# Experts sorted pair by pair, and a build-time scheduler with measured durations

## The chip, the cores and the metric

The kernel runs on one core of one Trainium2 chip, in float32 throughout. A core has TensorE (PE in the profile: matmuls and transposes, results in eight PSUM banks), VectorE (DVE), ScalarE (ACT), GpSimd (POOL) and SyncE (SP, which here only issues DMAs). The engines run their own instruction lists in order and meet at semaphores. The metric is the device time of one execution in microseconds (us), the median of several runs.

## The reference, cut to what matters

A tensor x of 16 sequences, 256 tokens each, 128 features, goes through four layers. Each layer normalises x, adds an attention, normalises again and adds a feed-forward part:

```
x = L0_attn_x                                    # (16, 256, 128)
x = x + L0_attn(ln(x)); x = x + L0_ffn(ln(x))    # 16 heads of 64, causal with distance bias, 2 null keys; gelu 128-512-128
x = x + L1_attn(ln(x)); x = x + L1_ffn(ln(x))    # 16 heads of 8, causal; gated 128-512, two 512-512 gelu layers, 512-128
x = x + L2_attn(ln(x)); x = x + L2_ffn(ln(x))    # 16 heads of 64, no mask; 8 experts
x = x + L3_attn(ln(x)); x = x + L3_ffn(ln(x))    # 16 heads of 8, causal, window 128; token shift and gates
```

The part that the change touches most is the third feed-forward layer, in which each token goes to the one expert with the highest gate value:

```
logits = xf @ gate_w.T + gate_b
top1 = argmax(logits, axis=-1)
for e in range(8):
    h = relu(xf @ w1[e].T + b1[e])
    y = h @ w2[e].T + b2[e]
    out = out + where((top1 == e)[:, None], y, 0)
```

## The kernel before

**A planner writes the order.** The source does not issue instructions as it goes along. It hands *steps* to a planner (class Plan, lines 66 to 219). A step has an engine, a rank p (a small number means wanted early), an assumed duration in ns, a function that emits its instructions, and the values that it reads (r), writes (w) or changes (m). run (line 129) then simulates the engines at build time and takes one step after the other; the order in which it takes them is the order in each engine's instruction list. Nothing is reordered on the chip. If a duration is assumed wrongly, the list is still correct, only the engine then waits.

What run looks at:

- A step can be taken when its inputs are there in the plan's time, and when its homes have a free place. A home is a set of buffers: "t" is the eight PSUM banks, "probs" six softmax tiles, "r" eight 128x512 tiles, "w" and "xs" three expert weight and row buffers, and so on. SEEN and TAIL add the delay between engines.
- Steps of a rank more than WINDOW = 12 beyond the *front* are held back. The front is the lowest rank of a PE step not yet taken (by_rank, line 132, and front, line 163).
- Among the steps that an engine could start within 40 ns of its earliest, it takes the lowest rank (line 190).
- PE steps have a mode: "T" is a plain full-array matmul or transpose, "S" and "O" use half-height or half-width tiles of the array, "S4" and "O4" quarter tiles. A step in another mode than the last counts SWITCH = 130 ns more (line 187).
- A copy out of a PSUM bank (evac, line 386; engine "AD") may run on ACT or on DVE. copies (line 377) gives the two assumed durations; whichever engine gets to it first in the plan takes it. Its rank is that of its matmul less 8.

**The layers.** Layer 0 has ranks from A0 = 0, 16 per sequence; layer 1 from A1, 12 per sequence; layer 2 from A2, 16 per sequence; layer 3 from A3, 12 per sequence. Layers overlap where ranks and data allow. In the layers with heads of 64 a sequence has four units (wide_unit, line 445) of four heads: scores (S), softmax on DVE and ACT, the division by the sum on POOL, transposes (T), products (O). In those with heads of 8 a sequence has three units (narrow_unit, line 532): scores (S4), first on DVE (line 553: adds the mask, takes the maximum, in one instruction per head and 128 queries), second on ACT (line 559: the exponential), transposes (T), products (O4). After each second sequence the feed-forward step of that pair follows; mix (line 1297) is that of layer 3.

**The experts.** Tokens are in two parts of eight sequences (four pairs) each; a part has its own sorted array of rows in DRAM. gate (line 1074) runs for each pair after its attention: it normalises into a tile of home "r", computes logits, a one-hot choice (oh), the count of earlier tokens with the same choice (ct), and on POOL a running total over the 128-token tiles (sofar). When all four pairs of a part are through, route (line 1121) runs once for the part: blocks_of works out how many blocks of 128 rows each expert needs and where they begin, places the row of each token (idx), owners the expert of each block (owni). Then 16 scatters (line 1157) on POOL, one per 128 tokens, write the normalised rows to their places in ex_rows by an indirect DMA. Then 23 blocks (line 1165): SP fetches the block's expert weights (line 1173) and rows (line 1174), PE transposes the rows (line 1178), two matmul steps with a relu between, and SP writes the result. Then 16 gathers on POOL (back, line 1205; indirect DMA at line 1210, addition at line 1215) bring the results back to x.

Their ranks, in experts (line 1234): part 0 route A2 + 153, scatters from A2 + 156, blocks from A2 + 178 every 2, gathers from A2 + 230; part 1 route A3 + 22, scatters from A3 + 23, blocks from A3 + 40 every 1.5, gathers from A3 + 70. The second part thus runs among the attention of layer 3, which begins at A3 with the first eight sequences; sequences 8 to 15 need the second part's gathers.

Of the kernel before, what the change touches and what calls it, by code (L numbers as in the profile page):

```python
# [15 lines left out]
P = 128  # L16
# [23 lines left out]
EX_PARTS = ((0, 4), (4, 8))  # L40
EX_BLOCKS = [4 * (z - a) + 7 for a, z in EX_PARTS]
# [25 lines left out]
class Plan:  # L67
# [5 lines left out]

    SEEN = {"PE": 80, "ACT": 60, "DVE": 60, "POOL": 110, "SP": 100}
# [54 lines left out]
    def run(self):  # L129
        free = dict.fromkeys(self.SEEN, 0.0)  # L130
        ready = {e: [] for e in free}
        by_rank = sorted((s for s in self.steps if s.eng[0] == "PE"), key=lambda s: (s.p, s.no))
# [27 lines left out]
        while left:  # L160
# [11 lines left out]
            for e, steps in ready.items():  # L172
                could = []
                for t, s in steps:
                    if s.p > front + window:
                        continue
                    k = places(s)
                    if k is None:
                        continue
                    t = max(t, k + self.SEEN[e] if k else 0.0, free[e])  # L180
                    could.append((t, s.p, s.no, s))
# [3 lines left out]
                if e == "PE":  # L185
                    low = min(c[1] for c in could if c[0] <= soon + 40)
                    could = [(t + (self.SWITCH if s.mode != mode else 0), p, n, s) for t, p, n, s in could
# [41 lines left out]
def preln_d4_kernel(ctx: ExitStack, tc: tile.TileContext, x_in, vecs, rows, bv2, nullk, nullv,  # L229
# [147 lines left out]
    def copies(n):  # L377
        return (0.83 * n + 42, 1.04 * n + 66)
# [11 lines left out]
    def layernorm(b, p, xn, at, times=1, behind=()):  # L390
# [22 lines left out]
        step("DVE", p, 560, stats, r=[X[b]], w=[ln])  # L413
        step("POOL", p, 980, scale, m=[ln])
# [119 lines left out]
    def narrow_unit(q, b, u, st, mask, mkey):  # L534
# [12 lines left out]
        for g in range(4):  # L547
# [14 lines left out]
            step("DVE", q + 1 + 0.7 * g, nh * (1.22 * w + 125), first, r=[s[g], mkey], w=[nm, pr, k])  # L562
# [81 lines left out]
    A0, A1, A2, A3 = 0, 4 * 4 * B, 4 * 4 * B + 4 * 3 * B, 4 * 8 * B + 4 * 3 * B  # L644
# [37 lines left out]
    step("DVE", -15, 800, null1, w=["nss"])  # L682
# [90 lines left out]
    def first0(p, u, k, bank, pr, j, nm):  # L773
# [5 lines left out]
        step("DVE", p, 730, f, r=[bank, f"bias{u}"], w=[pr, nm])  # L779
# [139 lines left out]
    def feed1(g):  # L919
        lo = A1 + 12 * (2 * g + 1) + 8 + 16  # L920
# [7 lines left out]
        for c in range(4):  # L928
# [14 lines left out]
            step("DVE", p - 8, 1270, gated, r=[pa, pb, "s1"], m=[th], w=[h[c]])  # L943
# [48 lines left out]
    def to_experts(e):  # L992
# [5 lines left out]
        for part in range(2):  # L998
            n = EX_BLOCKS[part]
            nt = n - 7  # L1000
            for name, shape, dt in (("oh", [nt, 8], F32), ("ct", [2, nt, 8], F32), ("sofar", [nt + 1, 8], F32),
                                    ("big", [n * 8], F32), ("nb", [3, 8], F32), ("pos", [nt], F32), ("idx", [nt], I32),
                                    ("own", [n], F32), ("owni", [n], I32)):
                late[name, part] = xq.tile([P] + shape, dt, tag=f"{name}{part}", name=f"{name}{part}x")
            nc.gpsimd.memset(late["sofar", part][:, 0, :], 0.0)

    step("SP", A1 + 70, 1000, to_w2, m=["wA"], w=["w2"], tail=15000)
    step("SP", A2 + 30, 1000, to_experts, m=["w1"], w=["late"], tail=4000)
# [5 lines left out]
    def prep2(b):  # L1014
        st = {}
        lo, hi = A2 + 16 * (b - 1), A2 + 16 * b - 2
# [45 lines left out]
    class Experts:  # L1062
# [12 lines left out]
        def gate(self, g, lo):  # L1075
# [24 lines left out]
            step("DVE", lo + 5, 1150, chosen, r=[ps, "late"], m=[lg], w=[oh, self.key("oh")])  # L1100
# [20 lines left out]
        def route(self, lo):  # L1121
            nt, nblk = self.nt, self.nblk

            def blocks_of(e):

                big, nb = self.tile("big"), self.tile("nb")
                c = big[:, 0:8 * nt].rearrange("p (e k) -> p e k", e=8)
                nc.vector.tensor_tensor(c, self.tile("sofar")[:, nt, :].unsqueeze(2).broadcast_to([P, 8, nt]),
                                        iota128[:, 0:nt].unsqueeze(1).broadcast_to([P, 8, nt]), ALU.is_gt)
                nc.vector.tensor_reduce(nb[:, 0, :], c, AX.X, ALU.add)  # L1130
                c = big[:, 0:64].rearrange("p (e k) -> p e k", e=8)
                nc.vector.tensor_tensor(c, before8, nb[:, 0, :].unsqueeze(1).broadcast_to([P, 8, 8]), ALU.mult)
                nc.vector.tensor_reduce(nb[:, 1, :], c, AX.X, ALU.add)
                nc.vector.tensor_tensor(nb[:, 2, :], nb[:, 0, :], nb[:, 1, :], ALU.add)
                nc.vector.tensor_scalar(nb[:, 1:3, :], nb[:, 1:3, :], float(P), None, ALU.mult)

            def places(e):
                cum = self.tile("ct")[:, 0, :, :]
                nc.vector.tensor_tensor(cum, cum, self.tile("sofar")[:, 0:nt, :], ALU.add)
                nc.vector.tensor_tensor(cum, cum, self.tile("nb")[:, 1, :].unsqueeze(1).broadcast_to([P, nt, 8]), ALU.add)  # L1140
                nc.vector.tensor_tensor(cum, cum, self.tile("oh"), ALU.mult)
                nc.vector.tensor_reduce(self.tile("pos"), cum, AX.X, ALU.add)
                nc.vector.tensor_copy(self.tile("idx"), self.tile("pos"))

            def owners(e):

                c = self.tile("big")[:, 0:8 * nblk].rearrange("p (j e) -> p j e", e=8)
                own = self.tile("own")
                nc.vector.tensor_tensor(c, iota128[:, 0:nblk].unsqueeze(2).broadcast_to([P, nblk, 8]),
                                        self.tile("nb")[:, 2, :].unsqueeze(1).broadcast_to([P, nblk, 8]), ALU.is_ge)  # L1150
                nc.vector.tensor_reduce(own, c, AX.X, ALU.add)
                nc.vector.tensor_scalar(own, own, 7.0, None, ALU.min)
                nc.vector.tensor_copy(self.tile("owni"), own)
# [287 lines left out]
```

## Time and profile before

| what | value |
|---|---|
| median of 3 runs | 2312.21 us (2311.94 to 2312.24) |
| the profiled execution's own time | 2310.75 us |
| its span, first to last instruction | 2309.1 us |
| PE busy | 2221.0 us, 96% |
| DVE busy | 1687.8 us, 73% |
| ACT busy | 1636.5 us, 71% |
| POOL busy | 1055.2 us, 46% |
| mean granted TensorE clock | 0.993 |

Busy time counts an engine as busy while an instruction of it is in flight. For PE that is not the same as working at its peak, since matmuls are pipelined and the ends are modelled. The stretches in which the layers mostly run are: layer 0 up to about 660 us, layer 1 to about 1190, layer 2 to about 1860 (experts of part 0 from 1607 to 1876), layer 3 to the end (experts of part 1 from 1937 to 2115).

### The profile page before, as it was taken

How to read it: one execution, taken by the hardware profiler on the slowest of the kernel's cores; microseconds unless marked ns; L12 is line 12 of the kernel's file. 1: busy time of each engine (PE TensorE's matmuls, PEld its weight loads, DVE VectorE, ACT ScalarE, POOL GpSimd, SP SyncE). 2: the span in 40 equal slices, each digit the busy share in tenths (PEclk: the TensorE clock that was granted, in tenths of full speed). 3: DMA queues.
4: the chain of work that ended last, by engine and by line, in shares of the span. 5: the costliest groups of instructions: out<-in, count | busy, mean ns of one | idle time of the engine just before them, and what ended most of it. 6: DMA issues, size and time to landing. Idle time of an engine off the chain costs nothing.

```text
span 2309.1 us, 50061 instructions
## 1 busy us (share of the span) xinstructions
PE 2221.0 (96%) x17039; PEld 1567.9 (68%) x17039; DVE 1687.8 (73%) x6308; ACT 1636.5 (71%) x4624; POOL 1055.2 (46%) x1985
## 2 busy tenths in 40 slices
PE   6999999999999999999999999999999999798996
PEld 3677666766776566565666677777788877586664
DVE  6898888888879665566655466767666679578996
ACT  5887877887879766677665565666665668567885
POOL 6887787877851111111112334445633483316321
PEclk9999999999999999999999999999999999899998
DMA  5000000000020000000000000000133100461000
GB/s 166 2 1 1 1 2 1 1 2 1 1 88 2 1 1 1 1 1 1 1 1 1 1 1 1 1 1 14 41 107 110 47 14 10 129 177 28 6 11 10
DMA packets 40895, 57.29 MB, mean 25 GB/s; under 512 B 4272, under 2 KB 31168, under 8 KB 40640
## 3 DMA queue, kind: packets, MB, share of 16 engines
q1 hardware_dynamic: 37840, 49.06, 7.0%
q0 software_dynamic: 2048, 4.20, 0.6%
q8 instruction: 136, 2.23, 0.4%
q10 hardware_dynamic: 752, 0.83, 0.1%
q14 instruction: 119, 0.97, 0.1%
HBM read 43.85 MB, written 10.22 MB: 23 GB/s over the span
## 4 chain that ended last, share of the span: by engine, by line
PE 75%; DVE 11%; POOL 8%; ACT 2%; issue 2%; DMA 1%; SPq 0%; POOLq 0%; DVEq 0%; ACTq 0%
PE t4x L366 8%; PE t2x L366 8%; PE t1x L366 8%; PE t0x L366 7%; PE t3x L366 7%; PE t5x L366 7%; PE t7x L366 7%; PE t6x L366 7%; PE t1x L484 1%; PE t5x L484 1%; PE t0x L484 1%; DVE probs4x L553 1%; PE t4x L484 1%; PE t2x L484 1%; PE t7x L484 1%
## 5 line engine op out<-in xcount | busy, mean ns | idle before, releaser
L441 POOL TENSOR_TENSOR x<-x,row_sb 128x256 f32<-128x256 f32 x48 | 35.1, 731 | 25.7 <-DVE xn2x L410 9.7
L473 POOL TENSOR_SCALAR probs2x<-probs2x,sums6x 128x256 f32<-128x256 f32 (+2 forms) x44 | 19.5, 459 | 47.8 <-DVE sums6x L468 25.3
L403 POOL TENSOR_SCALAR ln_rs2x<-ln_mv2x 128x2 f32<-128x2 f32 x22 | 4.6, 207 | 79.2 <-DVE ln_mv2x L399 78.5
L975 POOL TENSOR_TENSOR x<-x,sq1x 128x512 f32<-128x512 f32 x4 | 5.1, 1274 | 77.7 <-DVE sq1x L973 77.7
L370 POOL TENSOR_TENSOR ss2x<-ss2x,mhalf 128x16 f32<-128x16 f32 x11 | 33.1, 3010 | 15.5 <-DVE ss2x L728 12.0
L370 POOL TENSOR_TENSOR ss0x<-ss0x,mhalf 128x16 f32<-128x16 f32 x11 | 32.7, 2975 | 13.2 <-DVE ss0x L728 12.9
L403 POOL TENSOR_SCALAR ln_rs0x<-ln_mv0x 128x2 f32<-128x2 f32 x22 | 4.5, 207 | 74.7 <-DVE ln_mv0x L399 73.8
L473 POOL TENSOR_SCALAR probs0x<-probs0x,sums6x 128x256 f32<-128x256 f32 (+2 forms) x44 | 19.5, 457 | 36.6 <-DVE sums6x L468 36.4
L473 POOL TENSOR_SCALAR probs4x<-probs4x,sums6x 128x256 f32<-128x256 f32 (+2 forms) x40 | 17.6, 457 | 40.4 <-DVE sums6x L468 34.5
L473 POOL TENSOR_SCALAR probs4x<-probs4x,sums4x 128x256 f32<-128x256 f32 (+2 forms) x44 | 20.8, 487 | 32.2 <-DVE sums4x L468 19.5
L403 POOL TENSOR_SCALAR ln_rs4x<-ln_mv4x 128x2 f32<-128x2 f32 x23 | 4.7, 206 | 66.0 <-DVE ln_mv4x L399 65.0
L370 POOL TENSOR_TENSOR ss1x<-ss1x,mhalf 128x16 f32<-128x16 f32 x11 | 33.7, 3068 | 1.6 <-DVE ss1x L728 1.6
L370 POOL TENSOR_TENSOR ss4x<-ss4x,mhalf 128x16 f32<-128x16 f32 x10 | 29.8, 2980 | 10.1 <-DVE ss4x L728 8.2
L370 POOL TENSOR_TENSOR ss3x<-ss3x,mhalf 128x16 f32<-128x16 f32 x11 | 33.3, 3027 | 0.0
L403 POOL TENSOR_SCALAR ln_rs3x<-ln_mv3x 128x2 f32<-128x2 f32 x22 | 4.5, 206 | 62.0 <-DVE ln_mv3x L399 60.9
L473 POOL TENSOR_SCALAR probs4x<-probs4x,sums2x 128x256 f32<-128x256 f32 (+2 forms) x44 | 21.0, 492 | 25.6 <-DVE sums2x L468 20.4
L370 POOL TENSOR_TENSOR ss5x<-ss5x,mhalf 128x16 f32<-128x16 f32 x10 | 30.0, 2998 | 0.0
L975 POOL TENSOR_TENSOR x<-x,sq0x 128x512 f32<-128x512 f32 x4 | 5.1, 1279 | 54.4 <-DVE sq0x L973 54.4
L403 POOL TENSOR_SCALAR ln_rs1x<-ln_mv1x 128x2 f32<-128x2 f32 x23 | 4.7, 206 | 54.1 <-DVE ln_mv1x L399 53.0
L473 POOL TENSOR_SCALAR probs2x<-probs2x,sums2x 128x256 f32<-128x256 f32 (+2 forms) x44 | 20.8, 487 | 18.1 <-DVE sums2x L468 12.4
L473 POOL TENSOR_SCALAR probs0x<-probs0x,sums4x 128x256 f32<-128x256 f32 (+2 forms) x44 | 21.4, 500 | 15.5 <-DVE sums4x L468 15.5
L473 POOL TENSOR_SCALAR probs2x<-probs2x,sums4x 128x256 f32<-128x256 f32 (+2 forms) x40 | 19.5, 503 | 19.5 <-DVE sums4x L468 19.5
(4353 smaller groups left out, 10327.2 us busy)
## 6 DMA issues: line engine op xcount, KB each, us to landing
w0x<-in_wex_dram SPq DMA_DIRECT2D x16, 578.0 KB, 3.9
w1x<-in_wex_dram SPq DMA_DIRECT2D x15, 578.0 KB, 3.9
w2x<-in_wex_dram SPq DMA_DIRECT2D x15, 578.0 KB, 4.0
w_wA<-in_wa_dram SPq DMA_DIRECT2D x8, 512.0 KB, 6.9
ex_rows<-zero SPq DMA_DIRECT2D x2, 1472.0 KB, 10.3
x<-in_x_dram SPq DMA_DIRECT2D x8, 256.0 KB, 6.5
w_wB<-in_wb_dram SPq DMA_DIRECT2D x4, 512.0 KB, 7.5
ex_y<-bT1x SPq DMA_DIRECT2D x19, 64.0 KB, 3.4
```

Source lines behind the costliest of these rows:

```text
L366: nc.tensor.matmul(o, lhsT, rhs, start=start, stop=stop, **kw)
L370: nc.gpsimd.tensor_tensor(t, t, mhalf[:t.shape[0]].broadcast_to([t.shape[0], n]), ALU.pow)
L403: nc.gpsimd.tensor_scalar(ln.t[2], ln.t[1][:, :, 1], LN_EPS, 1.0, ALU.add, ALU.mult)
L441: step("POOL", p, 670, lambda e: nc.gpsimd.tensor_tensor(x_of(b), x_of(b), row_over(name, 2), ALU.add), m=[X[b]])
L473: nc.gpsimd.tensor_scalar(pr.t[:, j, a:z], pr.t[:, j, a:z], sums.t[:, i:i + 1], 1.0, ALU.mult, ALU.mult)
L484: nc.tensor.transpose(t.t[:, i * P:(i + 1) * P], probs[k // 2].t[:, k % 2, a:a + P], ident)
L553: nc.vector.tensor_tensor_reduce(pr.t[:, g % 2, c], s[g].t[:, c], m, -1.0, 3.0e38, ALU.add, ALU.min, nm.t[:, j:j + 1])
L975: step("POOL", lo + 30, 1300, lambda e: nc.gpsimd.tensor_tensor(x, x, ys.t.rearrange("p (c d) -> p c d", d=D), ALU.add), r=[ys, "w1"], m=xx)
```

## The change

Three things are done at once.

**The scheduler.** Steps of mode "T" no longer count for the front: it is the lowest rank of an S, O, S4 or O4 step not yet taken. A PE step of another mode is taken to start at the later of its own readiness and the engine's free time plus 130 ns; before, the 130 ns were added to its readiness. A copy that may run on either engine has its rank raised by SHY = 8 where DVE chooses (not where ACT does). Assumed durations change: copies, layer-norm statistics 560 to 788 ns, its scale 980 to 1070, first of the narrow units per instruction from 1.22 w + 125 to 1.04 w + 78 (for w = 256: 437 to 344; for w = 128: 281 to 211), first of layer 0 730 to 557, gated 1270 to 1380, the mix's difference 1300 to 1000, and one of 800 to 780.

**The sort.** route is replaced by place, which runs for each pair right behind its gate. State is kept between pairs in nb (9 rows of 8 numbers in place of 3) and own: blocks that each expert has so far, the end of all blocks so far, the block that each expert has open. A pair's tokens first fill the open block of their expert and go on in new blocks at the end. The number of blocks (23 a part) stays. A pair's four scatters follow its place at once.

**Ranks.** With first[l, b] the first rank of sequence b in layer l (the same numbers as before: A2 + 16 b, A3 + 12 b): place at first[2, b] + 29 and + 30, scatters at first[2, b] + 30, where b is the pair's second sequence. Blocks of part 0 from A2 + 157 (178 before) every 2, its gathers all at A2 + 207 (230 to 245 before). Blocks of part 1 from A3 + 29 (40 before) every 2 (1.5 before), its gathers all at A3 + 79 (70 to 85 before). Preparation of a sequence of layer 2 starts no earlier than 26 ranks before its end.

The diff, cut to its core:

```diff
+    SHY = 8
     SEEN = {"PE": 80, "ACT": 60, "DVE": 60, "POOL": 110, "SP": 100}
...
-        by_rank = sorted((s for s in self.steps if s.eng[0] == "PE"), key=lambda s: (s.p, s.no))
+        by_rank = sorted((s for s in self.steps if s.eng[0] == "PE" and s.mode != "T"), key=lambda s: (s.p, s.no))
...
-                    could.append((t, s.p, s.no, s))
+                    could.append((t, s.p + (self.SHY if e == "DVE" and len(s.eng) > 1 else 0), s.no, s))
...
-                    could = [(t + (self.SWITCH if s.mode != mode else 0), p, n, s) for t, p, n, s in could
+                    could = [(max(t, free[e] + self.SWITCH) if s.mode != mode else t, p, n, s) for t, p, n, s in could
...
-        return (0.83 * n + 42, 1.04 * n + 66)
+        return (0.83 * n + 54, 1.04 * n + 68)
...
-        step("DVE", p, 560, stats, r=[X[b]], w=[ln])
-        step("POOL", p, 980, scale, m=[ln])
+        step("DVE", p, 788, stats, r=[X[b]], w=[ln])
+        step("POOL", p, 1070, scale, m=[ln])
...
-            step("DVE", q + 1 + 0.7 * g, nh * (1.22 * w + 125), first, r=[s[g], mkey], w=[nm, pr, k])
+            step("DVE", q + 1 + 0.7 * g, nh * (1.04 * w + 78), first, r=[s[g], mkey], w=[nm, pr, k])
...
-        step("DVE", p, 730, f, r=[bank, f"bias{u}"], w=[pr, nm])
+        step("DVE", p, 557, f, r=[bank, f"bias{u}"], w=[pr, nm])
...
-        def route(self, lo):
-            nt, nblk = self.nt, self.nblk
+        def place(self, g, lo):
+            a, nt, nblk = 4 * (g - self.lo), self.nt, self.nblk
+            n, v = (g - self.lo) % 2, nc.vector
+            last = g == self.hi - 1
             def blocks_of(e):
+                nb, big = self.tile("nb"), self.tile("big")
+                had, has, new, begin, end, at, open_, step_, full = (nb[:, i, :] for i in (n, 1 - n, 2, 3, 4, 5, 6, 7, 8))
                 c = big[:, 0:8 * nt].rearrange("p (e k) -> p e k", e=8)
+                v.tensor_tensor(c, self.tile("sofar")[:, a + 4, :].unsqueeze(2).broadcast_to([P, 8, nt]),
+                                iota128[:, 0:nt].unsqueeze(1).broadcast_to([P, 8, nt]), ALU.is_gt)
+                v.tensor_reduce(has, c, AX.X, ALU.add)
+                v.tensor_tensor(new, has, had, ALU.subtract)
                 c = big[:, 0:64].rearrange("p (e k) -> p e k", e=8)
+                v.tensor_tensor(c, before8, new.unsqueeze(1).broadcast_to([P, 8, 8]), ALU.mult)
+                v.tensor_reduce(begin, c, AX.X, ALU.add)
+                v.tensor_scalar(begin, begin, end[:, 7:8], None, ALU.add)
+                v.scalar_tensor_tensor(open_, at, 1.0, had, ALU.add, ALU.subtract)
+                v.scalar_tensor_tensor(step_, begin, 1.0, at, ALU.subtract, ALU.subtract)
+                v.tensor_copy(full, had)
+                v.tensor_scalar(nb[:, 6:9, :], nb[:, 6:9, :], float(P), None, ALU.mult)
             def places(e):
+                nb = self.tile("nb")
+                over = lambda i: nb[:, i, :].unsqueeze(1).broadcast_to([P, 4, 8])
+                cum = self.tile("ct")[:, 0, a:a + 4, :]
+                past = self.tile("ct")[:, 1, a:a + 4, :]
+                v.tensor_tensor(cum, cum, self.tile("sofar")[:, a:a + 4, :], ALU.add)
+                v.tensor_tensor(past, cum, over(8), ALU.is_ge)
+                v.tensor_tensor(past, past, over(7), ALU.mult)
+                v.tensor_tensor(cum, cum, past, ALU.add)
+                v.tensor_tensor(cum, cum, over(6), ALU.add)
+                v.tensor_tensor(cum, cum, self.tile("oh")[:, a:a + 4, :], ALU.mult)
+                v.tensor_reduce(self.tile("pos")[:, a:a + 4], cum, AX.X, ALU.add)
+                v.tensor_copy(self.tile("idx")[:, a:a + 4], self.tile("pos")[:, a:a + 4])
             def owners(e):
+                nb, own = self.tile("nb"), self.tile("own")
+                new, begin, end, at, t = (nb[:, i, :] for i in (2, 3, 4, 5, 6))
+                v.tensor_tensor(end, begin, new, ALU.add)
+                v.tensor_scalar(new, new, 0.0, None, ALU.is_gt)
+                v.scalar_tensor_tensor(t, end, 1.0, at, ALU.subtract, ALU.subtract)
+                v.tensor_tensor(t, t, new, ALU.mult)
+                v.tensor_tensor(at, at, t, ALU.add)
+                v.tensor_scalar(t, end, float(P), None, ALU.mult)
                 c = self.tile("big")[:, 0:8 * nblk].rearrange("p (j e) -> p j e", e=8)
+                j, some = iota128[:, 0:nblk], self.tile("some")
+                v.tensor_tensor(c, j.unsqueeze(2).broadcast_to([P, nblk, 8]), t.unsqueeze(1).broadcast_to([P, nblk, 8]), ALU.is_ge)
+                v.tensor_reduce(some, c, AX.X, ALU.add)
+                v.tensor_tensor(own, own, some, ALU.add)
+                v.tensor_scalar(some, j, t[:, 7:8], -8.0, ALU.is_ge, ALU.mult)
+                v.tensor_tensor(own, own, some, ALU.add)
+                if last:
+                    v.tensor_copy(self.tile("owni"), own)
...
+            step("DVE", lo, 2100, blocks_of, r=[self.key("sofar")], m=[self.key("nb")])
+            step("DVE", lo, 1700, places, r=[self.key("nb"), self.key("oh"), self.key("sofar")], m=[self.key("ct")])
+            step("DVE", lo + 1, 2500, owners, r=[self.key("ct")], m=[self.key("nb")])
...
-            ex[g // 4].gate(g, A2 + 32 * g + 41)
+            e = ex[PART[g]]
+            e.gate(g, first[2, b] + 25)
+            e.place(g, first[2, b] + 29)
+            for t in range(4 * (g - e.lo), 4 * (g - e.lo) + 4):
+                e.scatter(t, first[2, b] + 30)
...
-    experts(0, A2 + 153, A2 + 156, A2 + 178, 2, A2 + 230)
-    experts(1, A3 + 22, A3 + 23, A3 + 40, 1.5, A3 + 70)
+    for e in ex:
+        lo = first[2, 2 * e.hi - 1] + 45
+        for j in range(e.nblk):
+            e.block(j, lo + 2 * j)
+        for t in range(e.nt):
+            e.back(t, lo + 2 * e.nblk + 4)
```

## The prediction

> **What bounds the kernel now.** I read the page first, then the busy time by stretch, then the list of waits, then the order of time around the longest wait.
>
> ```profile
> PE 2221.0 (96%) x17039; PEld 1567.9 (68%) x17039; DVE 1687.8 (73%) x6308; ACT 1636.5 (71%) x4624; POOL 1055.2 (46%) x1985
> PE   6999999999999999999999999999999999798996
> DVE  6898888888879665566655466767666679578996
> ```
>
> TensorE is in flight 96% of the time. The only thin slices are the first, the last, and two at about 1960 to 2080 us. So idle PE time is 88 us in all, and it is not spread evenly. The busy time by stretch, with these columns: length, then PE, PEld, DVE, ACT and POOL busy, granted clock, DMA share, GB/s:
>
> ```profile
> 50.00:660.00 610.00, 602.36 (x4341) 423.33 (x4341) 519.27 (x1893) 496.49 (x1493) 478.15 (x891) 1.00 0.01 1
> 660.00:1190.00 530.00, 524.24 (x3925) 329.98 (x3923) 355.20 (x1620) 379.17 (x874) 79.95 (x122) 1.00 0.03 11
> 1190.00:1860.00 670.00, 667.99 (x4676) 501.42 (x4675) 427.10 (x1020) 416.85 (x1345) 292.48 (x607) 1.00 0.10 29
> 1894.00:1979.20 85.20, 81.75 (x863) 58.37 (x861) 80.40 (x414) 72.96 (x188) 40.65 (x68) 1.00 0.06 15
> 1979.20:2027.00 47.80, 31.22 (x232) 27.28 (x232) 16.89 (x81) 17.79 (x53) 10.05 (x16) 0.82 0.55 170
> 2027.00:2119.00 92.00, 84.07 (x888) 67.62 (x886) 70.56 (x341) 64.69 (x173) 37.19 (x56) 1.00 0.39 111
> 2119.00:2273.00 154.00, 143.88 (x1526) 102.23 (x1526) 145.91 (x737) 126.39 (x331) 50.12 (x93) 1.00 0.03 9
> ```
>
> Layers 0, 1 and 2 keep PE at 99%. Layer 3 is different. Its attention alone (1894 to 1979, and 2119 to 2273) keeps **DVE** at 94 to 95%: 145.91 of 154.00 us. There DVE sets the pace, at 154/8 = 19.25 us a sequence with eight sequences in the stretch. PE would need less: the matmul records of that stretch have columns for 110 us at the 0.838 ns a column of back-to-back 512-column matmuls, 13.75 us a sequence. It also has 78 changes of array mode at about 0.2 us, another 1.95, so 15.7 in all. Between 1979 and 2027 no engine is full: DVE 35%, PE 65%. That is the hole, and it is opened by one wait:
>
> ```profile
> PE t1x L1178 <- DMA xs2x<-ex_rows: 12.2, 1, 12.2
> 1936.85 1.13 POOL L1161 DMA_INDIRECT ex_rows<-r0x,idx1x  x1 [9.07 <-DVE idx1x L1143]
> 1987.75 0.96 POOL L1161 DMA_INDIRECT ex_rows<-r5x,idx1x  x1 [1.53 <-DMA ex_rows<-r5x,idx1x]
> 1990.01 0.32 SPq L1174 DMA_DIRECT2D xs2x<-ex_rows  x1
> 1991.85 0.45 PE L1178 MATMUL t1x<-ident,xs2x 128*128 128x128 f32 x1 [12.24 <-DMA xs2x<-ex_rows]
> 1992.66 2.08 PE L366 MATMUL t2x<-bT0x,w2x 128*128 128x128 f32 x8 [0.36 <-ACT bT0x L382]
> ```
>
> The 16 scatters of part 1 run from 1936.85 to 1988.7, the last ones 2.5 us apart since each waits for the landing of the one before. SP can fetch the first block's rows only then. PE's list has that block's transpose next, with everything else behind it. After it the blocks run almost alone, some 3.2 us apart, because three weight buffers go round. And for a while PE is slow: eight 128-column matmuls took 2.08 us, against 1.06 at 2000.89.
>
> **The change part by part.**
>
> **Sort and scatter by pair.** In DVE durations I use the steps from start to start:
>
> ```profile
> 1926.61 0.41 DVE L553 CUSTOM_DVE_ANT_0 probs0x<-t4x,mask 128x256 f32<-128x256 f32 x1
> 1926.95 0.42 DVE L553 CUSTOM_DVE_ANT_0 probs0x<-t4x,mask 128x256 f32<-128x256 f32 x1
> 1935.09 0.29 DVE L1139 TENSOR_TENSOR ct1x<-ct1x,sofar1x 128x128 f32<-128x128 f32 x1
> 1935.42 0.29 DVE L1140 TENSOR_TENSOR ct1x<-ct1x,nb1x 128x128 f32<-128x128 f32 x1
> ```
>
> A 128-column operation costs 0.33 us; by the same reading a 64-column one 0.26, a 184-column one 0.38, a small one about 0.21. Then blocks_of is 2 x 0.33 + 2 x 0.26 + 6 x 0.21 = 2.4 us, places 8 x 0.22 = 1.8, owners 2 x 0.38 + 9 x 0.21 = 2.7: 6.9 us a pair, 55 for eight. Removed: 1.45 + 1.38 + 1.06 = 3.9 us a part, 7.8. Net +47 us of DVE. Six pairs fall into layer 2, where DVE is idle 36% of the time and PE is the bound: I cost them at +3 us for matmuls whose maxima queue behind them on DVE; without that cover they would be 41. Pair 6's gate is at about 1865, with DVE 71% busy, hidden. Pair 7 adds 6.9 - 3.9 = +3.0 us where DVE paces.
>
> The gain: pair 7's counts land at about 1924 in the trace, its running sum on POOL ends at 1925.8. Its blocks_of and places are 4.2 us of DVE, say 8 with the softmax work between. Four scatters at 2.5 us end at about 1945, the first rows are there at about 1949 instead of 1991.85. Meanwhile each pair's tile of home "r" is free early: mix needs seven of the eight, four of which part 1 holds until 1988 now.
>
> At this place one page speaks against the change: the Trainium skill, *SBUF — State Buffer*, section "SBUF: two separate sides", says that DVE and GpSimd share a port as an exclusive lock, and that an indirect DMA issued from GpSimd may starve while DVE holds it (620 ns becoming about 3100, in the section behind it). **Row:** the 32 scatters took 0.96 to 1.25 us each, the later 16 beside a DVE at 94%. By the rule's figure 32 scatters would cost 32 x 2.5 = 80 us of POOL; by the row nothing. I take the row.
>
> **Blocks and attention interleaved.** Blocks of part 1 come every 2 ranks over 46 ranks, that is 3.8 sequences of 12. With T steps out of the front a block that waits no longer holds the attention back. Over that stretch PE is the bound: 3.8 x 15.7 = 60 us of attention and 23 blocks at 1.83 us (a 128-column transpose and 16 matmuls at 0.107) + 0.4 for waits and mode changes = 51: 111 us. DVE needs 3.8 x 18.2 + about 12 = 81. At 4.8 us a block the 3.2 us of the weight ring is covered. The other 12.2 sequences stay paced by DVE: 12.2 x 19.25 = 235. With pair 7's 3.0: 349 us for what takes 2273 - 1894 = 379 now: **-30 us**. Of these the wait is 12.2 and the slow clock 3.4 (four groups of eight at twice 0.86). The rest is DVE working through the hole. The last 36 us are one chain and stay. Part 1's gathers, now in a row at A3 + 79, still have the stretch up to sequence 8 and follow blocks that end sooner.
>
> **Copies: SHY and durations.** In the last attention stretch DVE does 50 copies and ACT 68. DVE is 19.5 us busier; moving 16 copies at 0.6 would level them, 10 of 154 us, up to 15 over 12.2 sequences. Against that, first is now assumed at 4 x 0.211 x 4 + 2 x 4 x 2 x 0.344 = 8.9 us a sequence instead of 11.5. That is what the rows show (0.34 from 1926.61 to 1926.95), but it makes DVE look free to the planner, and may draw copies: +8. Between -15 and +8 I take **-4**, nearer the middle.
>
> **Mode price and durations in layers 0 and 1.** By columns these lose 610 - 535 and 530 - 484 us, 121 together. They have 430 mode changes; at a median of 0.165 us that is 71, so 50 are waits. Durations nearer the rows (first0 at 0.557, which is 0.35 + 0.21) may remove some: at best 25, at worst they add as much as the new mode rule costs. On this the skill, *TensorEngine Tiling*, section "Tiling Modes", under "Key Properties", says that changing the mode drains TensorE. **Row:** the records show 0.15 to 0.24 us lost in most changes. The new formula lets a wait swallow the 0.13. By the rule taken in full, 30% more changes would add 129 x 0.165 = +21 us; if the array has drained while PE waited, 0. I take 0 for that and a sixth of the 50 for the durations: **-8**.
>
> **Part 0's blocks and gathers** move 21 to 38 ranks forward inside layer 2, where PE is full with or without them: 0. Should layer 2 run short of T work at its end, PE there (33.81 of 34 us from 1860 to 1894) could lose 2 to 3 us.
>
> **The sum:** -30 - 4 - 8 + 3 = -39 us, from the profiled execution's own 2310.75 (span 2309.1) to 2271.8. The median of the runs lies 1.5 us above it: **2273 us**.
>
> **The rivals.**
>
> **Only the wait goes.** The 12.2 us and the 3.4 of slow clock vanish, but the list does not interleave well, or DVE takes the copies that it should lose: about 2312 - 16 = 2296. For it: layer 3 is DVE's already. Against it: DVE's 65% of idle time from 1979 to 2027.
>
> **DVE is relieved as well.** Copies level out in layers 1 and 3 (-15) and half the waits of layers 0 and 1 go (-25): -30 - 15 - 25 + 3 = -67, 2245. For it: durations that match the rows. Against it: PE there is in flight 99%.
>
> **Slower: banks come free later in layer 0.** A copy with its rank raised by 8 waits on DVE behind the next unit's softmax. Layer 0 has 289 copies on DVE, with ACT at 81%, DVE at 85%, POOL at 78%, so ACT cannot simply take them. If PE waits 0.2 us for each, +58: 2312 - 39 + 58 = 2331. It decides from 39/289 = 0.135 us a copy on. Against it: one 512-column copy is 0.6 us, and eight banks give some slack.
>
> **No effect.** The plan counts 980 + 2500 + 110 ns for a scatter that takes 2.5 us on the chip, and might put the blocks as late as before: 2312.
>
> **How the numbers follow.** My forecast 0.49 (its own range 2258 to 2288), only the wait 0.20, relief as well 0.16, slower 0.10, no effect 0.05. A measurement of this kernel can tell about 0.2% from no change, so faster is 0.85, same 0.05, slower 0.10. The range reaches from just under the relief case to above the wait-only case, 2240 to 2306, which leaves out slower, no effect, and the far tail of relief: 0.19.
>
> **What would show it.** Right: part 1's last scatter before 1950 and its first block within 5 us of it, no PE wait on ex_rows over 3 us, the clock at 1.00 throughout layer 3, blocks at least 4 us apart with quarter-tile scores between them, and layer 2 within 5 us of its length. Relief shows as fewer than 40 DVE copies in the last eight sequences. Wrong: the start of layer 3 moving by more than 15 us, which would mean that layers 0 to 2 decided; more than 900 mode changes in the span; or PE waiting for copies in layer 0.

## The result, and the profile after

The changed kernel takes 2276.16 us in the median (2274.31 to 2277.63, 4 runs), the kernel before, measured beside it, 2312.07 (2309.91 to 2312.24). The ratio is 0.9846, 95% interval 0.9829 to 0.9863: 36 us or 1.5% faster. The forecast was 2273, range 2240 to 2306. The total came out; its terms partly did not, and the experiments below show which.

The page of the changed kernel, its first part and two rows of slices:

```profile
PE 2210.3 (97%) x17039; PEld 1568.3 (69%) x17039; DVE 1688.1 (74%) x6436; ACT 1664.0 (73%) x4700; POOL 1051.9 (46%) x1989
PE   6999999999999999999999999999999999899997
DVE  5887888888878666666654557776766679898996
```

The matmuls are the same 17039. Of the two thin PE slices of before (a 7 and an 8 near the end) one is left, an 8; ACT is busy 27.5 us longer, and DVE as long as before.

To see where the time went I cut both executions at the same places of the work: at the first score matmul of layer 0, the last of layer 0, the first of layer 2, the first of layer 3, the first of sequence 8 in layer 3, and the last of all. What comes before the first cut (38.8 us before, 47.3 after) I call the start. Busy time by stretch of the kernel before; columns are length, then PE, PEld, DVE, ACT and POOL busy, granted clock, DMA share and GB/s:

```profile
38.80:668.80 630.00, 622.36 (x4474) 437.36 (x4475) 532.46 (x1938) 511.99 (x1545) 491.79 (x918) 1.00 0.01 1
668.80:1191.20 522.40, 516.64 (x3880) 323.02 (x3877) 351.74 (x1610) 373.60 (x851) 72.82 (x106) 1.00 0.03 11
1191.20:1894.10 702.90, 700.70 (x4925) 527.35 (x4921) 451.25 (x1075) 442.03 (x1439) 324.23 (x676) 1.00 0.10 28
1894.10:2119.20 225.10, 196.93 (x1978) 153.27 (x1977) 167.95 (x834) 155.54 (x413) 87.99 (x141) 0.96 0.30 87
2119.20:2273.70 154.50, 144.58 (x1534) 102.63 (x1534) 146.41 (x740) 126.89 (x332) 49.92 (x92) 1.00 0.03 9
2273.70:2309.10 35.40, 18.65 (x186) 13.39 (x178) 16.03 (x54) 11.04 (x24) 5.37 (x7) 0.77 0.06 16
```

The same stretches of the changed kernel:

```profile
47.30:662.80 615.50, 612.92 (x4468) 435.15 (x4467) 512.90 (x1909) 518.17 (x1562) 485.33 (x916) 1.00 0.01 1
662.80:1186.80 524.00, 519.54 (x3879) 324.11 (x3876) 352.61 (x1612) 372.30 (x849) 73.15 (x108) 1.00 0.03 11
1186.80:1900.90 714.10, 706.38 (x4923) 529.53 (x4919) 478.06 (x1235) 453.83 (x1466) 332.75 (x685) 0.99 0.09 29
1900.90:2108.10 207.20, 196.00 (x2038) 157.20 (x2037) 176.74 (x871) 159.18 (x424) 86.16 (x148) 0.97 0.30 91
2108.10:2236.00 127.90, 125.80 (x1420) 91.31 (x1420) 125.21 (x684) 123.58 (x324) 45.51 (x80) 1.00 0.04 10
2236.00:2275.70 39.70, 23.44 (x242) 17.49 (x236) 18.90 (x66) 16.80 (x42) 5.37 (x7) 0.80 0.05 14
```

So: the start +8.5 us, layer 0 -14.5, layer 1 +1.6, layer 2 **+11.2**, the first half of layer 3 -17.9, its second half **-26.6**, the end +4.3. The sum is -33.4, the difference of the two spans (2309.1 and 2275.7). In the second half DVE and ACT are now level, 125.21 and 123.58 us, where DVE had 146.41 and ACT 126.89. That stretch also holds less work: 1420 matmuls of 1534, the rest having moved to the stretches beside it. Layer 3 is therefore best taken as a whole: 415.0 us before, 374.8 after, -40.2. Of layer 0's 14.5 us, 5 are idle time of PE (length less busy: 7.6 us before, 2.6 after). The other 9.5 lie in time in which PE counts as busy, with the same matmuls at a granted clock of 1.00; what shortened them was not tested.

Two losses were not in the forecast. The first is at the very start. The list of waits of the changed kernel, and then PE's first matmul in its timeline:

```profile
PE t0x L369 <- DMA w_wC<-in_wa_dram: 18.9, 1, 18.9
```

```profile
18.86 3.62 PE L369 MATMUL t0x<-w_wA,nv_sb 128*32 128x128 f32 x16 [18.86 <-DMA w_wC<-in_wa_dram]
```

PE's list now begins with the product of the null values and the output weights (null3), and waits 18.9 us for weights that come late in the load order. Before, PE began at 9.23 us with the first sequence's transpose. The step has nothing to wait for in the plan, mode "T" and rank 2. While T steps counted for the front, the front stood at -13 or below and rank 2 was more than 12 beyond it; now the front is the first score step and null3 may go at once.

The second is in layer 2, when place runs for a pair. Three lines of PE's timeline in the changed kernel at pair 0 (others between them are left out):

```profile
1376.22 1.13 PE L369 MATMUL t3x<-xnT0x,w_wA 128*128 128x256 f32 x4
1379.40 0.56 PE L369 MATMUL t5x<-pT4x,V0x 128*64 128x256 f32 x1 [2.05 <-DVE Q1x L1047]
1380.19 0.63 PE L369 MATMUL t5x<-pT4x,V1x 128*64 128x256 f32 x1
```

A bank had to be emptied by a bias addition (Q1x) that stood on DVE behind place. After that gap of 2 us PE ran at half pace for 3 us (0.4 us from one such product to the next, 0.2 at full clock): from 1379.6 to 1383.0 the granted clock was 0.50. It was 0.50 once more in layer 2, from 1809.7 to 1816.5, 1.7 us behind a wait of 2.3 us for POOL.

The rows above give the size. PE's idle time in layer 2 is 7.7 us where it was 2.2, so 5.5 of the 11.2 us are waits. The 10.2 us at half clock, where there were none before, would make some 5 more if PE does half as much in them; that is an estimate.

### The profile page after: what moved, and what is told of

It is laid out like the page before. It is cut to its first block, busy times and chain, and to the rows that moved or that the text cites. A ratio compares the mean times of both kernels' runs of the same rounds, so it can differ in the third digit from the quotient of the medians.

```text
span 2275.7 us, 50321 instructions
## 1 busy us (share of the span) xinstructions
PE 2210.3 (97%) x17039; PEld 1568.3 (69%) x17039; DVE 1688.1 (74%) x6436; ACT 1664.0 (73%) x4700; POOL 1051.9 (46%) x1989
## 4 chain that ended last, share of the span: by engine, by line
PE 83%; DVE 9%; ACT 3%; POOL 3%; issue 2%; DMA 1%; SPq 0%; POOLq 0%; ACTq 0%; DVEq 0%
PE t7x L369 10%; PE t4x L369 8%; PE t3x L369 8%; PE t6x L369 8%; PE t0x L369 8%; PE t1x L369 8%; PE t2x L369 7%; PE t5x L369 7%; PE t6x L487 1%; PE t2x L487 1%; PE t0x L487 1%; PE t4x L487 1%; PE t3x L487 1%; PE t5x L487 1%; PE t7x L487 1%
## 5 line engine op out<-in xcount | busy, mean ns | idle before, releaser
L406 POOL TENSOR_SCALAR ln_rs0x<-ln_mv0x 128x2 f32<-128x2 f32 x26 | 5.0, 192 | 72.8 <-DVE ln_mv0x L402 71.9
L476 POOL TENSOR_SCALAR probs4x<-probs4x,sums0x 128x256 f32<-128x256 f32 (+2 forms) x40 | 17.5, 454 | 24.9 <-DVE sums0x L471 24.9
L476 POOL TENSOR_SCALAR probs2x<-probs2x,sums0x 128x256 f32<-128x256 f32 (+2 forms) x44 | 19.4, 456 | 20.1 <-DVE sums0x L471 18.2
```

The lines of the kernel that those rows point to most:

```text
L406: nc.gpsimd.tensor_scalar(ln.t[2], ln.t[1][:, :, 1], LN_EPS, 1.0, ALU.add, ALU.mult)
L476: nc.gpsimd.tensor_scalar(pr.t[:, j, a:z], pr.t[:, j, a:z], sums.t[:, i:i + 1], 1.0, ALU.mult, ALU.mult)
```

## The experiments

All times are medians, with the ratio to the kernel before and its interval. The table cuts each execution as above; L1+2 is layers 1 and 2 together, L3 is from its first score to the end; the last column is the copies out of banks that DVE and ACT did in the second half of layer 3.

| kernel | time | start | L0 | L1+2 | L3 | DVE, ACT copies |
|---|---|---|---|---|---|---|
| before | 2312.1 | 38.8 | 630.0 | 1225.3 | 415.0 | 51, 68 |
| the change | 2276.2 | 47.3 | 615.5 | 1238.1 | 374.8 | 27, 83 |
| sort_only | 2318.2 | 39.7 | 629.9 | 1250.8 | 396.2 | 54, 65 |
| sched_only | 2289.7 | 44.6 | 615.6 | 1228.9 | 398.6 | 27, 86 |
| shy_only | 2284.0 | 38.9 | 615.2 | 1227.3 | 401.3 | 17, 96 |
| shy0 | 2292.1 | 46.8 | 618.4 | 1239.3 | 386.3 | 54, 58 |
| old_dur | 2289.1 | 42.7 | 624.4 | 1238.5 | 381.8 | 13, 99 |
| old_switch | 2274.2 | 48.3 | 615.8 | 1231.3 | 377.1 | 26, 85 |
| front_t | 2276.6 | 37.6 | 618.1 | 1240.3 | 379.9 | 27, 86 |
| held_null | 2268.3 | 36.7 | 618.0 | 1236.6 | 374.6 | 27, 83 |
| placebo | 2277.7 | 48.0 | 615.7 | 1238.2 | 376.1 | 29, 81 |

**How much is chance.** Every edit of the planner makes a new list for all engines, so I asked what an edit without a reason does.

```diff
-        return (0.83 * n + 54, 1.04 * n + 68)
+        return (0.83 * n + 55, 1.04 * n + 69)
```

> The change with each copy assumed 1 ns longer: no reason, only another list (9283 lines of difference on PE). It tells how far a list may fall from another by chance. If the layers' times are those of the causes named: 2273 to 2280 and each layer within 3 us of the change. If the planner's lists scatter more: outside that, and differences of 5 us between variants mean nothing.

2277.66 us (0.985, 0.9834 to 0.9867), each part within 2 us of the change. This is a weaker test than it was meant to be. Compared place by place, by tiles without buffer numbers and by shapes, PE's list in the trace is the change's own in 16927 of 17039 matmuls, so the many differing lines must be buffer numbers for the most part. The run says how alike two nearly equal lists are, not how far a really different one falls by chance. A better hint is old_switch below: it moves 1516 places, shifts layers 1 and 2 by 7 us, and the total by 2. So I read differences of some 10 us and more, or smaller ones that a line of the trace explains.

**The sort alone.** sort_only is the change with the planner of before.

```diff
-        by_rank = sorted((s for s in self.steps if s.eng[0] == "PE" and s.mode != "T"), key=lambda s: (s.p, s.no))
+        by_rank = sorted((s for s in self.steps if s.eng[0] == "PE"), key=lambda s: (s.p, s.no))
...
-    SHY = 8
+    SHY = 0
```

(The mode formula and all assumed durations go back too.)

> The change with the planner as before: T steps in the front, the 130 ns added to readiness, no SHY, the old durations; only the sort by pair and the new ranks of the experts stay. If the gain is that of the early sort (no wait for ex_rows, blocks among the attention of layer 3): 2285 us (2278 to 2293), no PE wait on ex_rows over 3 us, first scores at 38.8 us as before. If the gain is the planner's: 2300 or more.

2318.22 us (1.0024, 1.0014 to 1.0035): **slower than before**. Layer 3 gains 18.8 us, and no wait on ex_rows stands among PE's longest; layer 2 loses 25. The two halves of layer 3, in the columns of above:

```profile
1920.40:2126.50 206.10, 191.20 (x1982) 150.89 (x1981) 174.35 (x849) 150.87 (x414) 77.30 (x132) 0.98 0.30 91
2126.50:2280.00 153.50, 144.29 (x1534) 102.68 (x1534) 146.52 (x739) 125.03 (x326) 48.99 (x90) 1.00 0.03 9
```

All of the gain is in the first half: 19.0 us, of which 13.3 are idle time of PE (28.2 to 14.9). The second half is as before, DVE and all. The sort is also what mixes blocks and attention: 11 of the 48 score steps of layer 3 (a score step is the scores of one unit) stand among part 1's blocks here, against 5 before and 2 in sched_only. My theory that the early sort makes the whole gain fell here. Its mechanism is there, at two thirds of its size, and its price in layer 2 is larger.

**The planner alone.** sched_only is the kernel before with the four edits of the planner.

> The kernel before with only the planner changed (front without T, new mode formula, SHY, new durations); the sort stays one per part, with the old ranks. If the sort makes the gain: 2300 us (2294 to 2310), part 1's scatters still until about 1985, a wait of PE on ex_rows that may be shorter since the front no longer holds back attention. If the planner makes the gain: 2288 or less, with layer 3 shorter by 25 us without the sort.

2289.73 us (0.9906, 0.989 to 0.9923), between the two expectations. Layer 3 gains 16.4 although part 1 is still sorted in one go, its last scatter at 1989. Layer 0 gains 14.4. For layer 3 the two halves of the change nearly add up: 18.8 + 16.4 = 35.2 of 40.2.

**Which part of the planner.** The kernel before with SHY alone, and the change without it:

```diff
-                    could.append((t, s.p, s.no, s))
+                    could.append((t, s.p + (self.SHY if e == "DVE" and len(s.eng) > 1 else 0), s.no, s))
```

> The kernel before with SHY = 8 and nothing else. If SHY is the cause of the shorter end of layer 3: last eight sequences 128 to 135 us, 2286 to 2292, first scores at 38.8. If it needs the durations: above 145 us and 2303 or more.

> The change with SHY = 0: DVE takes copies at their full rank again. If SHY is what moved the copies of layer 3 (51 on DVE in the last eight sequences before, 27 after) and shortened those sequences from 154.5 to 127.9 us: about 50 DVE copies, 145 to 155 us, 2296 to 2303. If the durations did that: below 35 copies, 130 us, 2274 to 2281.

shy_only: 2283.98 us (0.988, 0.9863 to 0.9896). **One line, without any sort, is 28 of the 36 us.** Half of it is in layer 0 (14.8 us), half in layer 3 (13.7). It is also 6 us faster than sched_only, which has the three other edits of the planner as well and loses those 6 us at the start. In the second half of layer 3 DVE's copies fall from 51 to 17 and the stretch from 154.5 to 137.8 us. shy0: 2292.06 us (0.9911, 0.9895 to 0.9928), 54 copies on DVE. The second half of layer 3 in the two, shy_only first, in separate fences:

```profile
2105.70:2243.50 137.80, 132.64 (x1504) 95.26 (x1508) 125.40 (x689) 133.18 (x351) 52.24 (x92) 1.00 0.03 10
```

```profile
2110.90:2253.20 142.30, 134.62 (x1473) 96.53 (x1474) 140.90 (x712) 119.84 (x313) 48.22 (x86) 1.00 0.03 9
```

With SHY and the old durations ACT is the fuller one (133.18 of 137.80); without SHY and with the new durations DVE is full to the last (140.90 of 142.30). Each overshoots on its own side. Both together give 125.21 and 123.58 of 127.90. Their effect is not additive elsewhere: layer 0 takes 615.2 with SHY alone, 618.4 without it, 615.5 with both. But SHY with the old durations, the new front and the new formula (old_dur, next) takes 624.4, so what makes layer 0 shorter is not one of the edits by itself, and stays open.

**The durations.**

> The change with the durations of before, SHY and the rest as changed. If SHY alone moves the copies: the last eight sequences stay near 130 us, 2276 to 2284. If the durations are needed: above 145 us there, 2295 or more. Layer 0 tells which of the two made it 14 us shorter after its start.

2289.1 us (0.9909, 0.9892 to 0.9925): 13 copies on DVE, 99 on ACT, layer 3 7 us longer and layer 0 9 us longer than with the change. The forecast of this run, below 2284 or above 2295, missed on both sides. Taken out of the change, the durations cost 13 us and SHY 16.

**Levelling, or the order of the lists.** If the gain in layer 3 is that DVE and ACT are level, more SHY must hurt, because ACT then sets the pace. shy16 has held_null (below) as its base.

```diff
-    SHY = 8
+    SHY = 16
```

> held_null with SHY = 16. In held_null DVE and ACT are level in the last eight sequences (125.2 and 123.6 of 127.9 us, 27 copies on DVE). If levelling is what shortened them, more is too much: fewer than 20 copies on DVE, ACT sets the pace, 130 to 138 us there and 2272 or more. If it is DVE's own order (softmax before copies) that helps: 2268 or less.

2276.44 us (0.9842, 0.9826 to 0.9859) against held_null's 2268.3: 20 copies on DVE, 92 on ACT, the second half of layer 3 at 138.9 us instead of 127.9, layer 3 as a whole 7 us longer. More SHY hurts, as levelling would have it, but not in the way that it would:

```profile
2099.40:2238.30 138.90, 131.72 (x1484) 95.97 (x1480) 132.22 (x686) 130.94 (x341) 46.97 (x80) 1.00 0.03 9
```

DVE and ACT, 132.22 and 130.94 us, are as level as in the change, and neither is full. The stretch also holds 64 matmuls more than the change's. To compare equal work I cut the traces once more, from the 31st to the 43rd of the 48 score steps of layer 3, four sequences:

| kernel | length, us | matmuls | DVE busy | ACT busy | DVE, ACT copies |
|---|---|---|---|---|---|
| before | 81.9 | 796 | 94% | 80% | 28, 34 |
| sort_only | 81.6 | 796 | 95% | 81% | 27, 34 |
| shy0 | 73.6 | 784 | 99% | 88% | 26, 34 |
| shy_only | 73.7 | 808 | 91% | 99% | 9, 55 |
| old_dur | 72.3 | 792 | 89% | 100% | 6, 55 |
| sched_only | 71.9 | 796 | 98% | 97% | 15, 47 |
| the change | 71.6 | 796 | 98% | 96% | 15, 47 |
| shy16 | 74.5 | 798 | 96% | 96% | 12, 51 |

Without SHY, shy0 has the copies of before and still gains 8 of the 10 us (7 if its 12 missing matmuls are allowed for). SHY alone gains no less with a third of DVE's copies. So where the copies go does not decide by itself; something else in the lists, such as the order of DVE's steps, which the durations change too, does nearly as much. The shortest times go with level engines, but old_dur is within 1 us of them with ACT full, and shy16, as level, is 3 us longer. How much is levelling and how much is order is not settled here.

**The mode formula and the front.** Each undone in the change:

```diff
-                    could = [(max(t, free[e] + self.SWITCH) if s.mode != mode else t, p, n, s) for t, p, n, s in could
+                    could = [(t + (self.SWITCH if s.mode != mode else 0), p, n, s) for t, p, n, s in could
```

> The change with the 130 ns of a mode change added to readiness as before. If the new formula matters little, as forecast: 2274 to 2280 and 785 to 800 mode changes in the span (795 before, 784 after). If it makes part of the gain: 2283 or more.

2274.19 us (0.9836, 0.9819 to 0.9852), 785 mode changes against 784: the new formula is worth nothing in total. Layers 1 and 2 are 7 us shorter with the old one, layer 3 is 2 us longer.

> The change with T steps in the front again, all else as changed. If the front rule only costs at the start and the sort alone lets blocks and attention mix: first scores at about 39, 2268 to 2274. If layer 3 needs the front rule to mix them: start 8 us sooner, layer 3 longer by 20 or more, 2285 or more.

2276.59 us (0.9841, 0.9825 to 0.9858). The start is back at 37.6, layer 3 loses 5 us, layers 0 to 2 lose 5. So the front rule has about the value of the start that it spoils, though 5 us here and there are within what a list may do by chance, and neither expectation was right as a whole.

**The start.** Would layer 0 have made up the 8.5 us anyway?

```diff
-    step("PE", 2, 2000, null3, w=[nv_ps], mode="T")
+    step("PE", 2, 2000, null3, r=["nkT"], w=[nv_ps], mode="T")
```

> The change, with one step of layer 0 (the products of the null values with the output weights, line 700) made to wait for the null keys, so that it no longer stands first in PE's list. If the 8.5 us by which the first scores of layer 0 come later (47.3 against 38.8) are lost for good: first scores before 40 and 2268 us (2265 to 2271). If layer 0 makes them up, since DVE, ACT and POOL are all near 85%: 2274 to 2278.

2268.3 us (0.9811, 0.9795 to 0.9827), first scores at 36.7. The loss is for good, and one added dependency takes it away: this is the fastest kernel of the study, 8 us faster than the change.

**The loss in layer 2.** I had two ideas, both tried on held_null. The first was that part 0's blocks, moved forward, leave layer 2 short of T work at its end.

```diff
-        lo = first[2, 2 * e.hi - 1] + 45
+        lo = first[2, 2 * e.hi - 1] + (45 if e.part else 66)
...
-            e.back(t, lo + 2 * e.nblk + 4)
+            e.back(t, lo + 2 * e.nblk + 4 if e.part else first[2, 0] + 230 + t)
```

> The change with the null values' step held back (as in held_null, 2268.3) and part 0's blocks and gathers at their old ranks (A2 + 178, A2 + 230 on). If the 6 us lost at the end of layer 2 come from blocks that are used up too early: the loss between the last score matmuls of layer 1 and those of layer 2 falls from 9.5 to about 3, and the time to 2262. If they come from the sort's DVE work: 2268.

2270.05 us (0.982, 0.9803 to 0.9836), and the first score of layer 3 comes at 1891.3 as in held_null. The idea is wrong. But the run shows the loss more plainly, since the blocks no longer blur it: against the kernel before it is 9 us ahead from pair 0 to 1860 us, and 2.9 ahead at 1891. In between lies place for pair 6. Some lines of DVE's timeline there, in held_late, and then of POOL's (start in us, duration in us, instruction):

```profile
1864.38 0.29 DVE L1147 TENSOR_TENSOR big0x<-sofar1x,iota 128x128 f32<-128x128 f32 x1 [2.63 <-POOL sofar1x L1129]
1873.96 2.76 DVE L1187 TENSOR_TENSOR big0x<-iota,nb1x 128x184 f32<-128x184 f32 x1
1877.86 0.48 DVE L1313 TENSOR_SCALAR q3x<-t6x,vec_sb 128x256 f32<-128x256 f32 x1
```

```profile
1873.73 0.92 POOL L476 TENSOR_SCALAR probs3x<-probs3x,sums1x 128x256 f32<-128x256 f32 x2
1874.62 1.88 POOL L531 TENSOR_TENSOR K2x<-q1x,owner 128x1024 f32<-128x1024 f32 x1
```

And the list of waits of held_late from 1840 to 1905 us (sum of the wait in us, times, longest):

```profile
PE t6x L369 <- DVE q3x L1313: 3.1, 1, 3.1
PE t0x L487 <- ACT probs4x L1067: 2.7, 1, 2.7
```

From 1864.4 to 1877.9 DVE does place and hardly anything else. One comparison of 184 columns, 0.35 us elsewhere, takes 2.76 and ends 0.2 us after a POOL operation does. PE waits 3.1 and 2.7 us in that time, and its clock falls to 0.74 from 1880 to 1885. The second idea was then that cutting place into small steps lets the softmax pass.

```diff
-            step("DVE", lo, 2100, blocks_of, r=[self.key("sofar")], m=[self.key("nb")])
+            if not last:
+                lo += 6
+            for ns, f in ((700, blocks_of), (1000, blocks_2), (850, blocks_3)):
+                step("DVE", lo, ns, f, r=[self.key("sofar")], m=[self.key("nb")])
```

(The other two functions are cut in the same way, into two and four. All but a part's last place also come six ranks later.)

> held_null (2268.3) with place cut into nine steps of two to four instructions instead of three of eight to eleven, and, but for a part's last pair, six ranks later. If the 7 to 8 us that the sort still costs in layer 2 (712.5 us there, 704.9 with the old sort and the same planner) come from matmuls whose maxima and biases queue on DVE behind a whole place: layer 2 at 705 to 708 us and a time of 2261 to 2265. If it is the amount of DVE work, drawn out by POOL on the shared port: no change, 2267 to 2270.

2269.1 us (0.9812, 0.9796 to 0.9829), no faster than held_null. At pair 0 the loss falls from about 2.4 to 0.5 us and layer 2 from 712.5 to 709.9, but the first half of layer 3 takes 3.5 longer. PE's idle time in layer 2 is halved, 9.6 us in held_null and 4.5 here, which is what the idea said; but the granted clock was 0.50 for 6.8 us of layer 2 here and at no time in held_null's. So standing behind place explains a good part of the waits, and the total does not show it. When the clock falls is not explained either: held_null has the two waits of 2.0 and 2.4 us too, and keeps its clock. What settles the rest of layer 2's loss stays open: with the sort layers 1 and 2 take 1231 us (old_switch) to 1251 (sort_only), without it 1225 to 1229, so the sort costs there in every list tried, but how much depends on the list.

## Why the prediction was right, and where its steps were not

| step | predicted | measured | shown by |
|---|---|---|---|
| sort: wait gone, blocks among attention (layer 3) | -30 | -18.8 | sort_only |
| copies and durations (layer 3) | -4, between -15 and +8 | -16.4 alone, -21 beside the sort, both with front and mode formula | sched_only; 374.8 - 396.2 |
| layers 0 and 1 | -8 | -4.4 with the start | the change: +8.5 - 14.5 + 1.6 |
| place in layer 2 | +3 | +11.2 | the change |
| end of layer 3 | 0 | in the layer 3 rows | |
| sum | -39 | -33.4 | |

**Right:** layer 3 was bound by DVE and one wait, and layers 1 and 2 by PE; the wait goes with the sort by pair. Layer 0, in flight 99% like them, was not at its floor: it lost 14.5 us. The last scatter starts at 1950.2, and PE waits on ex_rows 1.6 us once. Its first block is at 1956, 6 us on rather than 5. The port rule, weighed by the scatters, did not slow them (0.96 to 1.24 us each after): a price was paid on the other side, as shown above. Not all its other signs came: the last scatter is 0.25 us late, layer 2 is 11 us longer and not within 5, blocks come 4.7 us apart in the mean but down to 2.2, and the clock in layer 3 is not 1.00 throughout: ahead of its last chain it is 0.50 for 13.7 us, against 17.1 before. The sign given for relief, fewer than 40 copies on DVE in the last eight sequences, came (27). Two readings were a little off: the second thin PE slice runs from 2078 to 2136 us, and the last four of the 16 scatters fell into the hole, where DVE was at 35%, not 94.

**Mis-sized, the sort in layer 3.** Of the 30 us, 15.6 were the wait and its slow clock. If these came in full, the other 14, DVE working through the hole, shrank to about 3 in sort_only. I took 111 us for 23 blocks beside 3.8 sequences. In the changed kernel blocks take 1956 to 2060, 104 us, with ten units of attention in it, which is 3.3 sequences. And I costed the gathers at nothing. They now stand in a row on POOL, and sequence 8 waits for them; the timelines of POOL and PE of the changed kernel there:

```profile
2095.08 0.47 POOL L1255 TENSOR_TENSOR x<-x,yg1x 128x128 f32<-128x128 f32 x1
2095.64 0.19 POOL L406 TENSOR_SCALAR ln_rs2x<-ln_mv2x 128x2 f32<-128x2 f32 x1
2097.21 0.74 PE L426 MATMUL t2x<-ident,xn0x 128*128 128x128 f32 x2 [3.38 <-DVE xn0x L413]
```

PE waits 3.38 us for a normalised tile whose scale stood on POOL behind gathers and additions. From the last score step of the first eight sequences to the next one 24.5 us pass (2083.6 to 2108.1); in sort_only 18.0, before 9.0. That this is the whole of the missing 11 us was not tested.

**Mis-sized, the copies.** The bound of -15 in layer 3 was worked out by moving 16 copies in the kernel before. It held for SHY alone (-13.7), not for the planner's edits together, among which the front rule may be 5 us (front_t). The choice near the middle was the mistake: the balance of DVE and ACT, 146 against 127 us in a stretch of 154, was in the first table. The +8 for cheaper DVE durations that draw copies had the wrong sign. They draw copies beside SHY (13 in old_dur, 27 in the change), not without it (54 in sort_only and in shy0), and in both cases layer 3 is shorter with them: 381.8 to 374.8, and 396.2 to 386.3 together with front and formula. The rival "DVE is relieved as well" came nearer: it counted 15 us for the copies and 25 for the waits of layers 0 and 1, of which 12.9 came.

**Failed, the cover in layer 2.** The +3 rested on DVE being idle 36% of the time there. An average does not cover a block of 8 to 14 us in one place: PE's idle time there rose by 5.5 us, and fell again by 5.1 when place was cut into steps (split_place against held_null). A slow clock in layer 2 was not in the sum at all. I also weighed the shared port only for POOL; DVE was the one that waited.

**Missed, the start.** The front rule was read for what waits in layer 3, not for what it lets go first. Its mode price, taken as 0, was right: 784 changes against 795, and nothing in total in old_switch. Layers 0 and 1 alone gained 12.9 us against 8 forecast.

The errors offset each other: 11 us too much for the sort, 12 to 17 too little for the copies, 8 too little for layer 2, 8.5 for the start against 5 gained in layers 0 and 1. That the total came so near was in good part luck.

## What to carry to other kernels

Where two engines can do the same copies, look at the busy time of both in the stretch that they pace, and try to relieve the fuller one: here one line that made it the second choice was worth 28 of 36 us, and twice the dose gave 8 us back. Then compare stretches of equal work, since level engines alone did not tell the faster list from the slower one. A rule about what may go early must be read for every step that it frees, above all for the first of a list, where an in-order engine stands behind it with nothing to do. And when a change is several edits, forecast each by the stretch it acts in; a right total can hide terms that are wrong by half.

## What the runs showed of the hardware that was not expected

The same comparison of 128x184 on DVE, both inputs in SBUF, in all eight places of the changed kernel (nb0 is part 0, nb1 part 1):

```profile
L1187 DVE TENSOR_TENSOR big0x<-iota,nb0x x4: 349/350/352, 1377.5 to 1605.3; 128x184 f32<-128x184 f32 x4
L1187 DVE TENSOR_TENSOR big0x<-iota,nb1x x4: 351/469/2457, 1699.4 to 1940.9; 128x184 f32<-128x184 f32 x4
```

The columns after the count are the least, median and greatest duration in ns: about 350 in the six with no POOL operation beside them, 587 and 2457 in the two beside POOL's tensor operations. Small two-input ones of 128x32 took 191 ns where no POOL operation overlapped and 355 where a POOL scaling did (means of 29 and 19 in the trace). This fits the exclusive lock of the Trainium skill's *SBUF — State Buffer* ("SBUF: two separate sides"), seen from DVE's side. The page gives the lock to whichever operation starts first. By the recorded starts it was not so simple: the comparison of 2457 ns began at 1885.43 under a scaling that ended at 1885.82, and ended only at 1887.88, behind a second POOL operation that ran from 1885.79 to 1887.67. The scatters on POOL kept their 0.9 to 1.3 us.
